# Value products of two quads in one run, with single-quad value loads, in a cross-attention kernel on one core

## The chip, the cores and the metric

The kernel runs on one core of a Trainium2 chip. The core has a matrix engine (TensorE, "PE" in the profile; its weight loads are "PEld"), VectorE (DVE), ScalarE (ACT), GpSimd (POOL), and SyncE (SP), which here only issues transfers (DMAs). The engines run at the same time, each through its own list in order, and wait for one another by semaphores. The metric is the device time of one execution in microseconds (us), lower is better.

## The reference

Layer norm, cross-attention with 32 heads of 32 channels, output projection, residual; all in float32. B = 8 batches, S = 256 query rows, T = 256 context rows, D = 1024. The context serves as keys and as values, and is not projected.

```
x = (hidden - mean) * rsqrt(var + 1e-5) * gamma + beta
Q = split_heads(x @ Wq.T)                    # 8 x 32 x 256 x 32
K = V = split_heads(ctx)
scores = einsum('bhsd,bhtd->bhst', Q, K) * 32 ** -0.5     # masked with -inf
probs = softmax(scores)
attn = einsum('bhst,bhtd->bhsd', probs, V)
out = hidden + attn.reshape(B, S, D) @ Wout.T
```

## The kernel before

The work goes by quads: four heads, that is 128 channels, of one batch. There are 8 quads to a batch and N = 64 in all. The main loop runs over slots n = 0 to 63, and the order in which it issues instructions is the order on each engine; there is no scheduler (`manual_schedule`). What a slot puts on PE, in order:

1. the scores of quad n + 1 (L481, 16 instructions in the profile, into four PSUM banks),
2. steps of the output projection, "place 0" (`project_steps(n, 0)`),
3. the value products of quad n - 2 (L624): for each of four blocks of context rows, four heads and two halves of the rows, a matmul with 64 rows and 32 columns; 64 instructions in the profile, into two PSUM tiles `pv`,
4. steps, "place 1",
5. the query projection for a later quad (L342 in the first two batches; later one of seven block products a slot, L442, 32 instructions in the profile),
6. after the softmax has been issued, steps, "place 2".

The output projection of a batch is done while the next batch is worked on. It is a 2 x 2 block product in seven products (`PRODUCTS`: A11, A12, S2, ...) of four chunks each, 28 steps; a step is one matmul of 128 x 512 (L710), which the profile shows as two. `STEPS` says how many go into places 0, 1 and 2 of the nine slots in which the projection of a batch runs (the ninth is the first of the batch after). In `P1_ASIDE` batches the first product has a PSUM bank of its own. A step needs the attention outputs `at` of its quads, which ACT copies from `pv` (`copy_at`, L637).

In slot n the softmax of quad n + 1 is issued (`softmax_parts`). For each of the four heads DVE adds the mask and takes the minimum (L517), ACT makes the exponentials and their sum (L521), DVE the reciprocals (L528), POOL the scaling (L530), and DVE transposes blocks of 32 into `pT` (L536). ACT copies part of `pT` aside into `pc` (`aside`, L542). At the end stands `tail()`: the last transpose, the last copy aside, and then on SP two moves within `pT` (L602), the loads given as `between`, and two moves from `pc` into `pT` (L606). SP runs these in order: a load in `between` is issued after the moves of L602, which wait for the last copy aside. In the first eight and the last seven quads the tail is put off into the softmax that follows.

`copy_at` stands in the softmax after the first head's exponentials, or after the last head's where `late` is set.

Values are loaded for two quads at a time (`load_v`, 512 KB, two buffers, tile `v`): in an odd slot n for quads n + 1 and n + 2. Keys are loaded for two quads in an even slot (`load_k`, 256 KB). Slots and quads before the change:

```
        if n >= 2:
            values(n - 2)
...
        if n % 2 and n + 1 < N:
            between.append(partial(load_v, n + 1))
        elif n % 2 == 0 and n + 4 < N:
            between.append(partial(load_k, n + 4))
```

`ps_s` (scores) has four PSUM banks, `ps_v` (values) two, the query projection and the output projection one each.

## Time and profile before

| | us |
|---|---|
| median of 3 runs (572.2 to 574.37) | 572.57 |
| the profiled execution | 571.86 |
| its span | 570.1 |
| PE busy | 564.9 (99%) |
| DVE busy | 459.4 (81%) |
| ACT busy | 411.4 (72%) |
| POOL busy | 410.3 (72%) |
| value products, PE (L624, 4096 instructions) | 74.4 |
| scores, PE (L481, 1024 instructions) | 73.6 |

The columns of a timeline line are start, length, engine, line, operation, out<-in with shapes, and how many instructions were merged. Busy time of PE is counted from starts to modelled ends, so neighbouring runs overlap a little; from the start of one run to the start of the next is the cleaner measure of what a run costs. "to landing" of a DMA is from the start of its issue on the queue to the last part's arrival.

### The profile page before, as it was taken

What the parts mean: (1) busy time and instruction counts of PE and PEld (TensorE: products, weight loads), DVE (VectorE), ACT (ScalarE), POOL (GpSimd) and SP (SyncE); (2) the same over time, 40 slices, a digit from 0 to 9 for tenths busy, and PEclk for the clock granted to TensorE, in tenths of its full rate; (3) what the DMA queues carried; (4) which work ended last, traced back from release to release, by engine and by line L of the source; (5) the groups of instructions that cost most, each with busy time, mean ns of one, the idle gap of its engine ahead of it and who ended that gap; (6) DMA issues with size and microseconds to landing.
All of it is one profiled execution on the core that took longest, in us unless ns stands there. A gap on an engine that the chain in (4) does not pass through costs nothing.

```text
span 570.1 us, 19996 instructions
## 1 busy us (share of the span) xinstructions
PE 564.9 (99%) x7162; PEld 392.0 (69%) x7162; DVE 459.4 (81%) x1695; ACT 411.4 (72%) x1425; POOL 410.3 (72%) x677
## 2 busy tenths in 40 slices
PE   8999999999999999999999999999999999999997
PEld 8788885666667777667776777667766767755544
DVE  5897988797878888978898888988888877879823
ACT  4698887776768857787667867778766876769820
POOL 1788898899887896866569566677648657448780
PEclk9999999999999999999999999999999999999999
DMA  8973777756777767877788767886568864536751
GB/s 312 396 216 118 224 203 206 223 159 191 213 237 247 227 188 231 249 207 221 193 241 231 226 175 215 242 271 182 141 176 265 254 196 126 144 111 179 208 159 75
DMA packets 47475, 117.98 MB, mean 207 GB/s; under 512 B 9104, under 2 KB 9872, under 8 KB 47376
## 3 DMA queue, kind: packets, MB, share of 16 engines
q1 hardware_dynamic: 47088, 116.69, 68.5%
q8 instruction: 57, 0.93, 0.7%
q14 instruction: 42, 0.34, 0.2%
q10 hardware_dynamic: 288, 0.01, 0.0%
HBM read 65.28 MB, written 11.53 MB: 135 GB/s over the span
## 4 chain that ended last, share of the span: by engine, by line
PE 85%; POOL 6%; DVE 4%; issue 2%; ACT 1%; DMA 1%; DVEq 0%; POOLq 0%; ACTq 0%
PE po_S L710 19%; PE pq_A L442 16%; PE sc L481 11%; PE pv L624 10%; PE po_A L710 10%; PE pq L342 8%; PE pq_S L442 6%; POOL e L530 4%; PE po_end L777 2%; DVE e L517 2%; DVE pT L536 1%; PE po_last L777 1%; PE busy L120 1%; POOL wo L183 1%; ACT e L521 1%
## 5 line engine op out<-in xcount | busy, mean ns | idle before, releaser
L530 POOL TENSOR_SCALAR e<-e,rden 128x256 f32<-128x256 f32 x512 | 236.5, 481 | 116.7 <-DVE rden L528 114.4
L521 ACT ACTIVATE e<-e,mn 128x256 f32<-128x256 f32 x512 | 253.9, 501 | 50.4 <-DVE mn L517 49.3
L536 DVE STREAM_TRANSPOSE pT<-e 128x512 f32<-128x512 f32 x256 | 180.9, 707 | 46.4 <-POOL e L530 38.6
L517 DVE CUSTOM_DVE_ANT_0 e<-sc,mb 128x256 f32<-128x256 f32 x512 | 185.5, 416 | 29.3 <-PE sc L481 28.8
L542 ACT COPY pc<-pT 128x512 f32<-128x512 f32 x128 | 79.1, 618 | 67.2 <-DVE pT L536 38.9
L521 ACT ACTIVATION_READ_ACCUMULATOR e<-e,mn 128x1 f32 x512 | 97.8, 191 | 0.0
L342 PE MATMUL pq<-xnT,wq 128*128 128x256 f32 (+1 forms) x368 | 84.1, 383 | 0.0
L342 PEld LDWEIGHTS pq<-xnT,wq 128*128 128x128 f32 x368 | 68.7, 190 | 14.3 <-issue 4.3
L481 PEld LDWEIGHTS sc<-k,qa 32*128 32x128 f32 x1024 | 46.1, 184 | 42.0 <-issue 20.5
L710 PE MATMUL po_S<-wo,at 128*128 128x512 f32 x152 | 74.5, 607 | 0.4 <-DVE r L752 0.3
L624 PE MATMUL pv<-pT,v 64*32 64x128 f32 x4096 | 74.4, 274 | 0.0
L481 PE MATMUL sc<-k,qa 32*128 32x256 f32 x1024 | 73.6, 400 | 0.1
L624 PEld LDWEIGHTS pv<-pT,v 64*32 64x32 f32 x4096 | 57.0, 105 | 23.1 <-issue 12.5
L710 PE MATMUL po_A<-wo,at 128*128 128x512 f32 x128 | 59.5, 605 | 0.0
L710 PE MATMUL po_S<-wo,s 128*128 128x512 f32 x104 | 49.9, 605 | 0.0
L517 DVE DVE_READ_ACCUMULATOR2_ANT mn<- 128x1 f32 x512 | 42.7, 83 | 0.0
L528 DVE RECIPROCAL rden<-den 128x2 f32<-128x2 f32 x256 | 37.5, 147 | 5.0 <-ACT e L521 4.1
L442 PEld LDWEIGHTS pq_A<-xnT,wq 128*128 128x128 f32 x320 | 37.3, 192 | 4.8 <-issue 4.1
L710 PEld LDWEIGHTS po_A<-wo,at 128*128 128x128 f32 x128 | 22.9, 189 | 25.4 <-issue 24.5
L710 PEld LDWEIGHTS po_S<-wo,at 128*128 128x128 f32 x152 | 25.6, 190 | 20.8 <-issue 19.3
L442 PE MATMUL pq_A<-xnT,wq 128*128 128x128 f32 x320 | 37.3, 275 | 0.0
L637 ACT COPY at<-pv 128x128 f32<-128x128 f32 x128 | 26.2, 253 | 8.7 <-PE pv L624 8.7
(95 smaller groups left out, 610.7 us busy)
## 6 DMA issues: line engine op xcount, KB each, us to landing
v<-in_kv_dram SPq DMA_DIRECT2D x32, 512.0 KB, 4.2
pT<-pT SPq DMA_DIRECT2D x128, 128.0 KB, 2.5
pT<-pc SPq DMA_DIRECT2D x128, 128.0 KB, 4.1
ring<-kept_T SPq DMA_DIRECT2D x18, 512.0 KB, 5.4
k<-in_kv_dram SPq DMA_DIRECT2D x32, 256.0 KB, 4.2
x<-in_x_dram SPq DMA_DIRECT2D x14, 512.0 KB, 5.9
r<-in_x_dram SPq DMA_DIRECT2D x28, 256.0 KB, 4.5
out_dram<-r SPq DMA_DIRECT2D x28, 256.0 KB, 2.8
```

What stands on the lines that cost most here:

```text
L342: nc.tensor.matmul(pqs[n], wq[:, o, c, :], xnTs[b](c), start=(c == 0), stop=(c == NC - 1),)
L442: nc.tensor.matmul(pqs[b][:, o, :], w[:, c], x_[:, c], start=begins and o + c == 0, stop=c == NK - 1, skip_group_check=True,)
L481: nc.tensor.matmul(scs[n][j][:, s, :], qa[r, n % NQ, ts(s, P)], ks[n - n % 2][r, n % 2, :], start=True, stop=True,)
L517: nc.vector.tensor_tensor_reduce(out=e[:, s, :], in0=pss[j][:, s, :], in1=mbs[n // NQ], scale=1.0, scalar=NO_SCORE, op0=ALU.add, op1=ALU.m ...
L521: nc.scalar.activation(e[:, s, :], e[:, s, :], AF.Exp, bias=mn[:, s : s + 1], scale=-1.0, accum_out=den[:, s : s + 1],)
L528: nc.vector.reciprocal(rden, dens[j])
L530: nc.gpsimd.tensor_scalar(es[j][:, s, :], es[j][:, s, :], rden[:, s : s + 1], 1.0, ALU.mult, ALU.mult,)
L536: nc.vector.transpose(pT[:, :, :, j, :, :].rearrange("p a i s k -> p (a i) s k"), es[j].rearrange("p s (b t) -> p b s t", t=K),)
L542: nc.scalar.copy(pc[:, :, ts(j, 2)], pT[:, 1, :, ts(j, 2)])
L624: nc.tensor.matmul(pvs[n][r][j * HD : (j + 1) * HD], vs[n - n % 2][ts(r, 2 * K), i, ds(n % 2 * P + j * HD, HD)], pT[ts(r, 2 * K), :, i, j, ...
L637: nc.scalar.copy(ats[b, k][:, c, :, ts(r, 2), :], pv.rearrange("p a s k -> p s a k"))
L710: nc.tensor.matmul(po, operand(b, name)[:, c], wo[:, which, c], start=begins and c == 0, stop=c == NK - 1, skip_group_check=not begins,)
```

## The change

`values` takes one quad or two. In the odd slots 11 to 55 it runs quads n - 3 and n - 2 one after the other, into the two PSUM tiles, which hold both quads; the even slots 10 to 54 have no value products. Outside them quads run singly as before. `copy_at` copies two quads with one instruction for each half, and is put after the last head's exponentials wherever a pair is waiting. The values of a quad get a tile of their own (256 KB, two buffers), and `v_loads` says in which slot's `between` each is issued: it follows the slot that frees the buffer (`run_at[quad - 2]`), and is one later where that slot has the quad's own number and is one of the pairs'. For pairs from slot 13 on, the even quad q is so loaded in slot q + 1 and the odd quad q also in slot q + 1, and both are used in the pair's slot: q + 3 for the even, q + 2 for the odd. There are four `pT` buffers instead of three and two `pc` instead of three. The host lays each quad's values out together. `STEPS` has other counts in the same 28.

```diff
-    ptp = ctx.enter_context(tc.tile_pool(name="ptp", bufs=3))
-    asp = ctx.enter_context(tc.tile_pool(name="asp", bufs=3))
+    ptp = ctx.enter_context(tc.tile_pool(name="ptp", bufs=4))
+    asp = ctx.enter_context(tc.tile_pool(name="asp", bufs=2))
...
-        vs[n] = vp.tile([P, NI, 2 * P], F32, tag="v", name=f"v_{n}")
+        vs[n] = vp.tile([P, NI, P], F32, tag="v", name=f"v_{n}")
         nc.sync.dma_start(
-            vs[n], kv[b, g // 2, :, 2 * T :].rearrange("p (i v) -> p i v", i=NI)
+            vs[n],
+            kv[b, g // 2, :, ds(2 * T + n % 2 * NI * P, NI * P)].rearrange("p (i v) -> p i v", i=NI),
         )
...
     load_v(0)
+    load_v(1)
...
-            late = "p1" in hooks
+            late = "p1" in hooks or any(len(quads) > 1 for quads in pvs)
...
-    def values(n):
-        pvs[n] = [
-            ps_v.tile([P, 2, NS, K], F32, tag="pv", name=f"pv_{n}_{r}") for r in range(2)
+    def values(*quads):
+        pair = pvs[quads] = [
+            ps_v.tile([P, len(quads), 2, NS, K], F32, tag="pv", name=f"pv_{quads[0]}_{r}")
+            for r in range(2)
         ]
...
+        for at, n in enumerate(quads):
+            pT, v = pTs.pop(n), vs.pop(n)
+            for i in range(NI):
+                for j in range(NH):
+                    for r in range(2):
+                        nc.tensor.matmul(
+                            pair[r][j * HD : (j + 1) * HD, at],
+                            v[ts(r, 2 * K), i, ts(j, HD)],
+                            pT[ts(r, 2 * K), :, i, j, :, :],
+                            start=(i == 0), stop=(i == NI - 1),
+                        )
...
-    STEPS = ((0, 0, 0), (4, 0, 3), (0, 1, 2), (0, 2, 2), (0, 2, 1), (0, 1, 2), (0, 0, 3), (0, 1, 2),
-             (0, 2, 0))
+    STEPS = ((0, 0, 0), (4, 0, 2), (0, 2, 2), (0, 2, 1), (0, 3, 1), (0, 2, 0), (0, 1, 3), (0, 1, 1),
+             (0, 3, 0))
...
-            return STEPS[:1] + ((0, 6, 0), (0, 2, 0), (0, 4, 1), (0, 3, 1)) + STEPS[5:]
-        return STEPS[:1] + ((0, 7, 0),) + STEPS[2:] if b in P1_ASIDE else STEPS
+            return STEPS[:1] + ((0, 6, 0), (0, 2, 1), (0, 3, 1)) + STEPS[4:]
+        return STEPS[:1] + ((0, 6, 0),) + STEPS[2:] if b in P1_ASIDE else STEPS
...
+    PAIRS = range(NQ + 3, N - NQ, 2)
+    runs = {n: (n - 3, n - 2) for n in PAIRS}
+    for n in range(2, N):
+        if not PAIRS[0] - 1 <= n <= PAIRS[-1]:
+            runs[n] = (n - 2,)
+    run_at = {quad: n for n, quads in runs.items() for quad in quads}
+    v_loads = {}
+    for quad in range(2, N):
+        n = max(quad, run_at[quad - 2])
+        n += n == quad and n in PAIRS[:-1]
+        v_loads.setdefault(n, []).append(quad)
...
-        if n % 2 and n + 1 < N:
-            between.append(partial(load_v, n + 1))
-        elif n % 2 == 0 and n + 4 < N:
+        between += [partial(load_v, m) for m in v_loads.get(n, ())]
+        if n % 2 == 0 and n + 4 < N:
             between.append(partial(load_k, n + 4))
...
-        if n >= 2:
-            values(n - 2)
+        if n in runs:
+            values(*runs[n])
```

More of the change, by code (lines that the diff above doesn't have):

```diff
@@ L614, in softmax_parts, with copy_at @@
         yield
-    def values(n):
-        pvs[n] = [
-            ps_v.tile([P, 2, NS, K], F32, tag="pv", name=f"pv_{n}_{r}") for r in range(2)
-        ]
-        pT = pTs.pop(n)
-        for i in range(NI):
-            for j in range(NH):
-                for r in range(2):
-                    nc.tensor.matmul(
-                        pvs[n][r][j * HD : (j + 1) * HD],
-                        vs[n - n % 2][ts(r, 2 * K), i, ds(n % 2 * P + j * HD, HD)],
-                        pT[ts(r, 2 * K), :, i, j, :, :],
-                        start=(i == 0), stop=(i == NI - 1),
-                    )
-    def copy_at(n):
-        b, c = divmod(n, NQ)
+    def values(*quads):
+        pair = pvs[quads] = [
+            ps_v.tile([P, len(quads), 2, NS, K], F32, tag="pv", name=f"pv_{quads[0]}_{r}")
+            for r in range(2)
+        ]
+        for at, n in enumerate(quads):
[9 more added lines that the diff above has]
+                        )
+    def copy_at(quads):
+        b, c = divmod(quads[0], NQ)
         k, c = divmod(c, NK)
@@ L635, in copy_at @@
             ats[b, k] = atp.tile([P, NK, NS, NA, K], F32, tag="at", name=f"at_{b}_{k}")
-        for r, pv in enumerate(pvs.pop(n)):
+        for r, pv in enumerate(pvs.pop(quads)):
             nc.scalar.copy(
-                ats[b, k][:, c, :, ts(r, 2), :], pv.rearrange("p a s k -> p s a k")
+                ats[b, k][:, ds(c, len(quads)), :, ts(r, 2), :],
+                pv.rearrange("p c a s k -> p c s a k"),
             )
@@ L980, in xattn_kernel @@
         else:
-            copy_at(n - 2)
+            copy_at((n - 2,))
             for load in between:
@@ L1057, in xattn_kernel @@
     values(N - 2)
-    copy_at(N - 2)
+    copy_at((N - 2,))
     end_sum(slice(2, 3), nc.gpsimd)
@@ L1065, in xattn_kernel @@
     values(N - 1)
-    copy_at(N - 1)
+    copy_at((N - 1,))
     end_sum(slice(3, 4), nc.vector)
@@ L1106 @@
     keys = keys.transpose(0, 1, 3, 2, 4).reshape(B, D // 256, P, 2 * T)
-    values = v.reshape(B, T // 64, 64, D // 256, 256).transpose(0, 3, 2, 1, 4)
+    values = v.reshape(B, T // 64, 64, D // 256, 2, P).transpose(0, 3, 2, 4, 1, 5)
     values = np.tile(values.reshape(B, D // 256, 64, 4 * T), (1, 1, 2, 1))
```

## The prediction

> **What bounds the kernel now.** First the page: busy times, the slices and the chain that ended last. TensorE (PE) is busy 99% of the span in every slice, at full granted clock, and it is 85% of the chain; no other engine is over 81%.

> ```profile
> span 570.1 us, 19996 instructions
> PE 564.9 (99%) x7162; PEld 392.0 (69%) x7162; DVE 459.4 (81%) x1695; ACT 411.4 (72%) x1425; POOL 410.3 (72%) x677
> PE   8999999999999999999999999999999999999997
> PE 85%; POOL 6%; DVE 4%; issue 2%; ACT 1%; DMA 1%; DVEq 0%; POOLq 0%; ACTq 0%
> ```

> Next the waits of PE alone: they are 2.0 us in all. So the time is the length of PE's own list, and every wait that is put into it is added whole.

> ```profile
> PE busy L120 <- POOL ring masks.py:199: 1.3, 1, 1.3
> PE po_end L777 <- ACT at L637: 0.4, 1, 0.4
> PE po_S L710 <- DVE r L752: 0.3, 1, 0.3
> ```

> Third the timeline of two slots, 28 (even) and 29 (odd), all engines (start, length, what). Slot 28 issues the scores of quad 29 at 254.09. Their softmax ends with the second copy aside (262.86, to 263.49), after which the DMA queue (SP) sends its first moves of the probabilities at 263.52. That is 9.43 us after the scores, and by then PE has begun slot 29 (262.60) and is about to start its value products (263.67). The load that stands between the two pairs of moves, here keys, goes out at 264.71.

> ```profile
> 254.09 1.15 PE L481 MATMUL sc<-k,qa 32*128 32x256 f32 x16
> 255.17 1.16 PE L624 MATMUL pv<-pT,v 64*32 64x128 f32 x64
> 256.25 1.98 PE L710 MATMUL po_S<-wo,at 128*128 128x512 f32 x4
> 258.07 3.73 PE L442 MATMUL pq_A<-xnT,ring 128*128 128x128 f32 x32
> 261.64 1.02 PE L710 MATMUL po_S<-wo,at 128*128 128x512 f32 x2
> 262.60 1.15 PE L481 MATMUL sc<-k,qa 32*128 32x256 f32 x16
> 262.86 0.63 ACT L542 COPY pc<-pT 128x512 f32<-128x512 f32 x1
> 263.52 1.15 SPq L602 DMA_DIRECT2D pT<-pT  x2
> 263.67 1.16 PE L624 MATMUL pv<-pT,v 64*32 64x128 f32 x64
> 264.71 0.58 SPq L136 DMA_DIRECT2D k<-in_kv_dram  x1
> ```

> Last the tile of the keys, whose loads have the size (256 KB) that a value load will have. The line is from the start of the issue to the landing, over 32 loads; 9.1 is the first microseconds of the program, the later ones are 2.8 to 6.2.

> ```profile
> DMA to landing us min/median/max: 2.8/4.2/9.1
> ```

> **The change, part by part.** The sum is made against the profiled execution: span 570.1, its own time 571.86; the median shown, 572.57, is 0.7 higher.

> *Two quads in one run.* From start to next start a scores run costs 1.08 (254.09 to 255.17) and a values run 1.085. The records inside a values run show eight rounds of eight matmuls, 0.109 apart, so 0.873 is work and 0.21 is entering and leaving it. In 23 odd slots (11 to 55) the second quad follows in the same shape: 23 x 0.21 = 4.9 us less. Bounds: nothing, if a run of 128 is limited by issue (late rounds already show single matmuls 0.017 apart, 0.133 for eight), and 4.9. I take 4.9, because the round starts stay 0.109 apart to the end of the run.

> *Steps dealt anew.* One step is two matmuls in the profile, 0.855 us (14 of them take 6.21). Each batch keeps its 28, so nothing is gained or lost; they only level the slots. With 1.08 for scores, 3.57 for a query product and 0.2 for changing shapes, an even slot becomes 1.08 + 4 x 0.855 + 3.57 + 0.2 = 8.27 (7.41 in the first slot of a batch, which has 3), an odd one 8.4 to 9.4. The A12 steps in the third slot now need attention copies that ACT makes after the last exponential: done some 7 us after the odd slot's scores, needed after 8.4 + 1.08. Cover 2.4 us, cost nothing.

> *Copies.* 128 copies of 128 columns (253 ns) become 36 of those and 46 of 256 (nearest row 463 ns, an activation): ACT is 72% busy and nobody waits for it here, so nothing. *Four probability buffers, two copies aside*: with two, the buffer is rewritten about 12 us after its transfers were issued, and those land in 4.1. Nothing.

> *Values by single quads.* This is the part that costs. The even quad of a pair is loaded in the odd slot two before its use. The odd quad q is loaded in slot q + 1, between the moves of the softmax of quad q + 2, and used in slot q + 2. So values of quad 27 are to be loaded where the timeline has keys, at 264.7, by a queue that must first send the moves of quad 29, and are wanted in slot 29, whose run begins at 263.67. The order of SP's queue in the changed program says the same: the load stands directly behind those two moves. Counted from the scores of the even slot:
> - moves sent after 9.74, 9.30, 9.43, 9.34 us in the first, third, fifth and seventh slot of a batch (slots 32, 34, 28, and the end of the copy aside in slot 30),
> - 1.2 for the two issues (263.52 to 264.71), 4.2 to land, 0.1 to restart PE: 5.5;
> - wanted after the even slot, the scores and the first quad of the odd one: 8.27 + 1.08 + 0.87 = 10.22 (first slot 9.36).

> The second quad therefore waits 5.88, 4.58, 4.71 and 4.62 us: 19.8 per batch. Pair 11 has its load a slot earlier; the pairs in 13 to 55 wait, two in the first batch and four in each of five: 9.3 + 99.0 = 108 us. It doesn't shrink from pair to pair, for the next scores stand behind the waiting run on PE and the next load hangs on those scores. Also behind it are the odd slot's steps and product; ACT's two copies of the pair stand ahead of its copies aside, so the odd slot's moves come some 5 us later too, but what they carry is used two slots on. Bounds: a landing of 2.8 gives 22 x 1.4 = 31 less, one of 6.2 gives 44 more; 4.2 is the middle of the same kind of load at the same place in the queue.

> Outside the pairs every single load goes out one slot ahead instead of two. At the end the moves of quad 57 start at 504.57 and the values of quad 56 at 508.97: 504.57 + 1.15 + 4.15 is 0.9 too late. Followed through slots 56 to the end, each wait shifting what comes after, this is about 5 us. At the start (moves at 55.96, wanted at 59.12) it is 2.1 once, about 3 in all, between 1.5 and 5.

> *The clock after a wait.* In the first records of PE 18 matmuls start 0.213 apart and then 0.109: after the idle start it ran at half speed for 3.9 us and lost 18 x 0.104 = 1.9. No row shows PE idle for 4 to 6 us in the middle; waits up to 0.4 left the clock whole. So 0 to 22 x 1.9 = 42 us. The waits lie between the two rows and I take half, 21. [...]

> [...]

> **Sum**: 571.86 - 4.9 + 108 + 5 + 3 + 21 = 704.

> **Rivals.**
> - *On the other side: the values are there in time.* Then only the shape changes count: 571.9 - 4.9 = 567, or 572 if a long run is issue-limited. It decides where moves are sent earlier than 10.22 - 5.4 = 4.8 us after the scores. For it: SP and the DMA queues are not full. Against it: the softmax's last exponential alone ends 6.0 after the scores, in every slot.
> - *No clock loss*: 684. For it: three waits in four are only about 4.6 us, and the first quad's work ends just before each. *Clock lost each time*: 725. For it: the slow start in this trace.
> - *The softmax loop is dragged along*: ACT's copies of the pair wait for the late run and its copy aside and product evacuation come after, at about 13 to 15 us; where this runs into the next even slot's exponentials it delays the moves there too. By the slots' lengths the overlap is 0.2 to 0.4 us in one or two slots of a batch; if it were a whole copy and read (1.3) each time, 22 x 1.3 = 29 more: 733.

> **How the numbers follow.** Late values 0.92: with part of the clock 0.42 (704), without loss 0.25 (684), with all of it 0.17 (725), dragged loop 0.08 (733). In time 0.07 (567 to 572; faster 0.06, within 0.5% 0.01); something that hides nearly all of it 0.01. Low end: 684 with a landing of 2.8 is 653, and 3 less at both ends of the program, 650. High end: 733 with 1.4 us slower landings in each pair, 765. About 0.5% is what a measurement of this kernel can tell from no change.

> **What would show it.** Right: PE's waits list values (L144) or the DMA of v ahead of the value products, 22 times, 4 to 6 us, some 100 us; PE busy near 85%; in the timeline of an odd slot 64 matmuls, a hole, then 64 more, the v load issued about 10.6 us after the even slot's scores. Shape: two quads back to back where nothing waits (slot 11) take 1.96 instead of 2.17. Clock: matmul starts 0.213 apart after the holes, or not. Wrong: runs of 128 without a hole, v landing before 10 us, or a hole whose end is a copy or a probability move instead.

## The result and the profile after

The changed kernel takes 724.09 us (median of 4 runs, 721.64 to 729.01) against 573.17 for the kernel before (4 runs, 572.2 to 574.37): 1.264 times, 95% interval 1.257 to 1.271. The predicted 704 is 20 us short of it; 650 to 765 holds it. The profiled execution has a span of 719.8 us, 149.7 more than before.

Three lines of the page after (span; busy time; busy tenths of PE and of its granted clock in 40 slices), and the shares of the chain that ended last:

```profile
span 719.8 us, 19981 instructions
PE 611.4 (85%) x7162; PEld 420.6 (58%) x7162; DVE 456.7 (63%) x1695; ACT 410.6 (57%) x1379; POOL 410.7 (57%) x677
PE   9998989779976887878978797779777887879988
PEclk9999999989988989999889999889998988999999
PE 65%; DMA 13%; POOL 6%; DVE 5%; issue 4%; ACT 4%; SPq 3%; DVEq 0%; ACTq 0%; POOLq 0%
```

PE has the same 7162 matmuls, yet its busy time grew by 46.5 us and its granted clock is 0.922 in the mean, which was 1.000: the matmuls themselves became longer. The other 103 us of the 149.7 are idle time, and DMA has 13% of the chain, which was 1%. PE's waits say for what (total, times, longest):

```profile
PE pv L628 <- DMA v<-in_kv_dram: 64.7, 17, 5.0
PE pv L628 <- issue: 18.7, 4, 5.8
PE pv L628 <- DMA pT<-pT: 8.9, 2, 5.0
PE pv L628 <- DMA pT<-pc: 4.4, 1, 4.4
PE po_S L715 <- DVE r L757: 3.0, 1, 3.0
```

The first four rows are one thing: all 24 waits stand in front of value products, 17 put down to the values' own load, the rest to whatever event came last by the profile. One odd slot (25) on PE and on SP (start, length, what; idle time ahead in brackets):

```profile
270.61 1.15 PE L483 MATMUL sc<-k,qa 32*128 32x256 f32 x16
271.69 1.16 PE L628 MATMUL pv<-pT,v 64*32 64x128 f32 x64
276.80 2.06 PE L628 MATMUL pv<-pT,v 64*32 64x128 f32 x64 [3.96 <-DMA v<-in_kv_dram]
278.79 5.90 PE L715 MATMUL po_A<-wo,at 128*128 128x512 f32 x12
284.62 1.15 PE L483 MATMUL sc<-k,qa 32*128 32x256 f32 x16
...
272.71 1.15 SPq L604 DMA_DIRECT2D pT<-pT  x2
273.90 0.58 SPq L144 DMA_DIRECT2D v<-in_kv_dram  x1
```

The first quad of the pair runs at 271.69. Only at 272.71 can SP send the moves of the next softmax, at 273.90 the load of the second quad's values, and at 276.80 PE goes on. Then its 64 matmuls take 2.06 us instead of 1.16, and the steps behind them 5.90 instead of 5.42 for the same twelve in e18.

For every run the span can be cut at two places, the start of the scores of quad 13 (slot 12) and of quad 57 (slot 56):

| kernel | time | ratio [95%] | start to 13 | 13 to 57 | 57 to end |
|---|---|---|---|---|---|
| before | 573.17 | 1 | 113.7 | 378.2 | 78.2 |
| after | 724.09 | 1.264 [1.257, 1.271] | 121.9 | 511.1 | 86.8 |
| e1 load in slot q | 596.19 | 1.041 [1.037, 1.044] | 122.9 | 380.4 | 87.8 |
| e2 the late load ahead of the moves | 621.29 | 1.085 [1.083, 1.088] | 120.4 | 411.4 | 87.9 |
| e8 e1, all loads ahead | 590.82 | 1.034 [1.030, 1.038] | 119.6 | 387.3 | 80.5 |
| e7 hole filled | 686.68 | 1.200 [1.195, 1.205] | 122.1 | 476.0 | 88.6 |
| e9 hole half filled | 711.65 | 1.242 [1.238, 1.246] | 123.1 | 501.2 | 88.5 |
| e5 single loads, no pairs | 579.72 | 1.012 [1.011, 1.013] | 120.0 | 377.5 | 80.3 |
| e13 e8, moves of x later | 596.68 | 1.042 [1.039, 1.045] | 114.9 | 398.7 | 80.2 |
| e15 loads on POOL | 581.87 | 1.016 [1.015, 1.018] | 118.0 | 382.6 | 79.3 |
| e16 five slots' loads on POOL | 583.53 | 1.019 [1.016, 1.022] | 118.2 | 385.0 | 79.1 |
| e17 nine slots' loads on POOL | 583.80 | 1.020 [1.015, 1.026] | 115.0 | 391.7 | 79.1 |
| e11 loads on ACT | 580.48 | 1.013 [1.007, 1.019] | 115.7 | 383.2 | 79.1 |
| e18 e11, S2 later everywhere | 571.91 | 0.998 [0.997, 1.000] | 115.3 | 375.5 | 79.1 |

Times are medians; one of e9's four runs (718.93) fell into a slower state of the chip and is left out. The last three columns are of one profiled execution each. Ratios are against runs of the kernel before on the same chip.

### The profile page after: what moved, and what is told of

It reads as the page before. It is cut to its first block, busy times and chain, and to the rows that moved or that the text cites. A ratio compares the mean times of both kernels' runs of the same rounds, so it can differ in the third digit from the quotient of the medians.

```text
span 719.8 us, 19981 instructions
## 1 busy us (share of the span) xinstructions
PE 611.4 (85%) x7162; PEld 420.6 (58%) x7162; DVE 456.7 (63%) x1695; ACT 410.6 (57%) x1379; POOL 410.7 (57%) x677
## 4 chain that ended last, share of the span: by engine, by line
PE 65%; DMA 13%; POOL 6%; DVE 5%; issue 4%; ACT 4%; SPq 3%; DVEq 0%; ACTq 0%; POOLq 0%
PE po_S L715 15%; PE pq_A L444 12%; PE pv L628 8%; PE po_A L715 8%; DMA v<-in_kv_dram 7%; PE pq L344 6%; PE sc L483 6%; PE pq_S L444 5%; POOL e L532 3%; DMA pT<-pT 3%; SPq L604 3%; DVE pT L538 2%; DVE e L519 2%; PE po_end L782 2%; ACT e L523 1%
## 5 line engine op out<-in xcount | busy, mean ns | idle before, releaser
L538 DVE STREAM_TRANSPOSE pT<-e 128x512 f32<-128x512 f32 x256 | 180.8, 707 | 48.1 <-POOL e L532 46.5
L628 PE MATMUL pv<-pT,v 64*32 64x128 f32 x4096 | 92.3, 317 | 100.9 <-DMA v<-in_kv_dram 64.7
L628 PEld LDWEIGHTS pv<-pT,v 64*32 64x32 f32 x4096 | 72.0, 121 | 122.2 <-issue 64.1
L715 PE MATMUL po_S<-wo,at 128*128 128x512 f32 x152 | 82.0, 660 | 0.0
L715 PE MATMUL po_A<-wo,at 128*128 128x512 f32 x128 | 65.5, 656 | 0.0
L641 ACT COPY at<-pv 128x256 f32<-128x256 f32 (+1 forms) x82 | 22.4, 324 | 73.9 <-PE pv L628 73.9
L715 PE MATMUL po_S<-wo,s 128*128 128x512 f32 x104 | 61.4, 720 | 3.0 <-DVE r L757 3.0
L715 PEld LDWEIGHTS po_S<-wo,at 128*128 128x128 f32 x152 | 28.5, 210 | 27.6 <-issue 27.2
L444 PEld LDWEIGHTS pq_A<-xnT,wq 128*128 128x128 f32 x320 | 39.2, 199 | 7.2 <-issue 6.0
L715 PEld LDWEIGHTS po_A<-wo,at 128*128 128x128 f32 x128 | 25.3, 209 | 30.5 <-issue 28.8
```

The source lines that it names most:

```text
L444: nc.tensor.matmul(pqs[b][:, o, :], w[:, c], x_[:, c], start=begins and o + c == 0, stop=c == NK - 1, skip_group_check=True,)
L538: nc.vector.transpose(pT[:, :, :, j, :, :].rearrange("p a i s k -> p (a i) s k"), es[j].rearrange("p s (b t) -> p b s t", t=K),)
L628: nc.tensor.matmul(pair[r][j * HD : (j + 1) * HD, at], v[ts(r, 2 * K), i, ts(j, HD)], pT[ts(r, 2 * K), :, i, j, :, :], start=(i == 0), sto ...
L641: nc.scalar.copy(ats[b, k][:, ds(c, len(quads)), :, ts(r, 2), :], pv.rearrange("p c a s k -> p c s a k"),)
L715: nc.tensor.matmul(po, operand(b, name)[:, c], wo[:, which, c], start=begins and c == 0, stop=c == NK - 1, skip_group_check=not begins,)
```

## The experiments

**e1: is it the slot of the load?** The line that puts the odd quad's load one slot later is dropped; pairs, tiles and steps stay.

```diff
         n = max(quad, run_at[quad - 2])
-        n += n == quad and n in PAIRS[:-1]
         v_loads.setdefault(n, []).append(quad)
```

> The one edit: the odd quad of a pair is loaded one slot earlier, in slot q instead of q + 1, still behind the moves. Theory of the late load: it lands some 15 us after the scores of slot q and is wanted after 18, so the holes inside the 22 runs go, and the slow clock with them: 132.9 us less between the scores of quads 13 and 57, and the pairs' 4.7 us show as a gain. The waits of the singly loaded quads at the start (8.2 us) and the end (8.6) stay in part: about 575 to 583 us, 1 to 2% slower than before. Rival, that the pair's probabilities or its copies are what is late: the holes stay, over 700 us.

596.19 us. Of the 151 us lost, 128 come back with this line. The holes are gone from most of the middle slots, and there one sees what a pair is worth. Odd slot 27 and 29 on PE:

```profile
253.82 2.03 PE L628 MATMUL pv<-pT,v 64*32 64x128 f32 x128
255.79 1.98 PE L715 MATMUL po_S<-wo,s 128*128 128x512 f32 x4
...
270.41 1.15 PE L483 MATMUL sc<-k,qa 32*128 32x256 f32 x16
271.49 0.80 PE L628 MATMUL pv<-pT,v 64*32 64x128 f32 x38
```

The run of 128 costs 255.79 - 253.82 = 1.97. Slots 28 and 29 together take 16.80 instead of 17.02. But the kernel is still 23 us slower than before, and the expectation was missed: 9.2 us are lost at the start, 9.6 at the end (slot 56 alone takes 15.99 instead of 9.37), and the middle, which should have gained 4.9, loses 2.2. In slots 25, 33, 41 and 49 value products still wait (10.4, 10.0, 10.7 and 9.0 us where 8.5 is undisturbed). On SP the loads for slot 25 are sent at 234.05, behind twelve moves of x (L331; the last six are shown) and more, and slot 25 starts at 234.12:

```profile
227.41 3.77 SPq L331 DMA_DIRECT2D xnT<-xe  x6
231.28 0.52 SPq L758 DMA_DIRECT2D out_dram<-r  x1
232.21 1.78 SPq L604 DMA_DIRECT2D pT<-pT  x2
234.05 1.07 SPq L144 DMA_DIRECT2D v<-in_kv_dram  x2
```

These two loads were put into slot 23, which had begun on PE at 218.16. So they go out 15.9 us after the start of their slot; in slot 27, where no moves of x are in the way, it is 11.5.

**e2 and e8: is it the place in SP's list?** In e2 the slot stays as in the change, and the pairs' late load goes ahead of the moves; in e8 e1's slot is taken and all value loads go ahead.

```diff
 e2
+        early = [m for m in v_loads.get(n, ()) if run_at.get(m) == n + 1 and n + 1 in PAIRS]
...
+        ahead = [partial(load_v, m) for m in early] + ahead
 e8
-        n += n == quad and n in PAIRS[:-1]
...
+        ahead = [partial(load_v, m) for m in v_loads.get(n, ())] + ahead
```

> The odd quad's load stays in slot q + 1, but is put on the DMA queue ahead of that slot's moves instead of behind them. Theory of the place in the queue: the load goes out as soon as the previous slot's transfers are issued, some 2 to 5 us after the even slot's scores instead of 10.5, lands by 5 to 9 us, before 10.23 where it is wanted; holes gone but for a few where six moves of x stand ahead; 575 to 590 us. Rival, that one slot is too short for the load wherever it stands: holes of 2 us or more in most pairs, over 640 us.

> The load of the odd quad in slot q, and every value load ahead of the slot's moves, the single ones at the start and the end too. Theory of the late loads: no value product waits, PE is the bound again, and what is left of the change is 23 pairs at 0.21 us: 571.9 - 4.8 = 567 us, faster than before by 0.8% (565 to 569). Rival, that a run of two quads is limited by issue and gains nothing: 572. Rival, that the dealt steps, the later copies or fewer copies aside cost something of their own: 573 to 580, with waits of PE for ACT or DVE.

621.29 and 590.82: both missed, in the same manner. In e2 the pairs that follow the third and fifth slots of a batch have their undisturbed 9.4 and 8.5 us in all but slots 37 and 43 (10.7 and 10.3), so there the moves of the probabilities had been the whole cause. The pairs that follow the seventh slots take 13.1 to 16.4 (but for slot 55, which has 8.6), because the queue is then late with moves of x that belong to slots before. Slot 23 on PE in e2:

```profile
221.43 1.16 PE L628 MATMUL pv<-pT,v 64*32 64x128 f32 x64
227.12 2.06 PE L628 MATMUL pv<-pT,v 64*32 64x128 f32 x64 [4.54 <-DMA v<-in_kv_dram]
```

In e8 the load for slot 25 is out at 231.93 and wanted at 233.8, again behind the moves of x (226.78, 4.15 long); slot 25 takes 12.71 and slot 49 14.43. So the first theory, "the load stands behind two moves", holds only for the place that the prediction looked at. The load is also behind everything else that SP has not yet sent.

**e7 and e9: what does the clock cost?** Between the two quads, nine (e7) or four (e9) matmuls of 128 x 256 keep PE busy while it would wait.

```diff
+            if at and n > 9:
+                for _ in range(9):        # e9: 4
+                    nc.tensor.matmul(
+                        banks[0][:, 256:512], wo[:, B11, 0, :P], wo[:, B11, 0, 0:256],
+                        start=True, stop=True, skip_group_check=True,
+                    )
```

> The changed kernel, with nine matmuls of 256 columns that nobody reads put between the two quads of each run from slot 11 on, about 4.0 us, nearly the length of the hole. They take no part in the result. Theory, that some 40 us of the loss are the clock halved after the hole: the loads land when they did, but PE stays at full clock, about 38 us less than the changed kernel: 683 to 692 us, granted clock 0.98 or more. Rival, that the slow stretch after the hole is PE's restart or late operands and not the clock: no less than 720 us. If the hole were not what sets the pace, the nine would add 4.0 x 23 = 92 us: 815.

> As the kernel with nine unread matmuls, but four of them, 1.9 us, put between the two quads; 2 to 3.5 us of idle time remain. The matmuls take no part in the result. If the clock falls only after an idle stretch of more than about 3.3 us (the shortest hole after which the changed kernel ran slow was 3.4, the longest after which it did not 3.6), nearly all pairs keep it: as with nine, 684 to 692 us, granted clock above 0.98. If any idle stretch of 2 us or more cools the array, it stays near 715 to 724.

e7 takes 686.68. The values come no earlier (the holes of the 22 pairs add up to 103.4 us, after the change to 98.5), so 724.1 - 686.7 = 37 us are what the slow clock cost, or somewhat more. The page of e7 shows the full clock in every slice (0.997 in the mean):

```profile
span 686.7 us, 20773 instructions
PEclk9999999999999999999999999999999999999999
```

e9, 711.65, gives back only 12 and stands beside the second of its two expectations. With e7 as the measure (from the start of the second quad to the next scores 6.53, 7.53, 6.56 and 6.56 us in the pairs that follow the first, third, fifth and seventh slot), the pairs from slot 13 on, without slot 17, which has four steps ahead of its quads, can be sorted by how long PE idled. In e9: up to 2.0 us, none of 4 lost anything; 2.1 to 2.9 us, 6 of 10 did; 3.0 and more, 7 of 7. Whoever lost, lost 1.5 to 2.7 us. After the change 20 of 21 lost, 1.3 to 2.8 each, 39.7 in all. Three pairs of e9 (slots 35, 53 and 27):

```profile
385.23 1.25 PE L637 MATMUL pv<-pT,v 64*32 64x128 f32 x64 [1.53 <-DMA v<-in_kv_dram]
386.41 1.98 PE L724 MATMUL po_S<-wo,s 128*128 128x512 f32 x4
...
592.90 1.96 PE L637 MATMUL pv<-pT,v 64*32 64x128 f32 x64 [2.12 <-DMA v<-in_kv_dram]
594.79 2.75 PE L724 MATMUL po_S<-wo,at 128*128 128x512 f32 x4
...
295.51 1.78 PE L637 MATMUL pv<-pT,v 64*32 64x128 f32 x64 [3.33 <-DMA v<-in_kv_dram]
297.22 3.05 PE L724 MATMUL po_S<-wo,s 128*128 128x512 f32 x4
```

After 1.53 us the run and its steps have their usual 1.2 and 1.98. After 2.12 and 3.33 they have 2.0 and 2.8, or 1.8 and 3.1. The one that lost nothing after the change (slot 27, below) had idled 3.30, so no single length decides:

```profile
298.42 1.23 PE L628 MATMUL pv<-pT,v 64*32 64x128 f32 x64 [3.30 <-DMA v<-in_kv_dram]
299.59 1.98 PE L715 MATMUL po_S<-wo,s 128*128 128x512 f32 x4
```

What does decide can be read from the granted clock. In every trace here it changes only at points that lie whole multiples of 3.41 us apart. Cut into such stretches, e9 around its wait of 2.12 us and the change around its wait of 3.30 us look like this (the stretch and its length; busy time of PE, PEld, DVE, ACT and POOL with instructions; PE's granted clock; DMA's share and GB/s):

```profile
589.54:592.95 3.41, 1.29 (x13) 0.84 (x16) 2.79 (x15) 2.82 (x12) 2.83 (x7) 1.00 0.64 195
592.95:596.36 3.41, 3.41 (x66) 2.29 (x67) 0.67 (x1) 1.17 (x3) 3.29 (x4) 0.50 0.34 85
...
293.44:296.85 3.41, 1.69 (x76) 1.09 (x68) 2.79 (x16) 3.41 (x11) 0.63 (x2) 1.00 0.89 274
296.85:300.26 3.41, 1.84 (x66) 1.40 (x67) 0.11 (x2) 2.40 (x10) 0.55 (x2) 1.00 0.81 257
300.26:303.68 3.42, 3.42 (x25) 2.70 (x24) 1.59 (x5) 0.08 (x1) 1.14 (x3) 1.00 0.04 12
```

The 2.12 us lie inside one stretch and leave PE idle for 62% of it, and the next stretch runs at half clock; the 3.30 us are shared by two stretches, 51% and 46% idle, and the clock stays full. Over all 14 traces, from 12 us on, a stretch at full clock that PE idled for more than 56% was followed by half clock every time (53 times, 22 of them after the change), and one that it idled for less than 52% never was; of four between, two were. So a wait of 1.78 us in e5 (its stretch 52% idle) cost the clock, and one of 2.81 us in e9 (slot 25) did not.

**e5: single loads alone.** The kernel before with each quad's values loaded by themselves in slot q, between the moves, without pairs and with the old steps and buffers.

```diff
...
-        if n % 2 and n + 1 < N:
-            between.append(partial(load_v, n + 1))
-        elif n % 2 == 0 and n + 4 < N:
+        if n >= 2:
+            between.append(partial(load_v, n))
+        if n % 2 == 0 and n + 4 < N:
```

> The kernel before, with only the loads changed: values by single quads, two buffers of 256 KB, quad q loaded in slot q and used in slot q + 2; runs of one quad, old steps, old buffers. Theory: in the middle the load lands 15 us after the scores of quad q + 1 and is wanted after 18, so nothing there; where the softmax's tail is put off or late (quads 3 to 6, 56 to 62) it waits, and where six moves of x fill the DMA queue, as e1 and e2 showed. So 578 to 592 us, waits ahead of value products 8 to 20 us in all, none above 4. Rival, that singles are early enough and all waits of the changed kernel come from the pairs: 572.

579.72. The middle is as before (377.5 against 378.2; 8.51 a slot): two loads in place of one, two slots ahead, cost nothing there, and the waits that the moves of x were expected to make did not come. The loss is at the start, 6.3 (slot 5 takes 11.02 instead of 7.54), and at the end, 2.1. So single loads explain part of the losses at both ends, and nothing in the middle. Of the 8.2 us that the change lost at the start, 4.0 are a step of S2 (below), and of its 8.6 at the end most stand in slot 56, which e5 leaves at 9.37.

**e13, e15, e16, e17: a better place for the loads.** All four load the values of a pair in the odd slot before it, as e8 does, and have S2's first step in slot 10 back where the kernel before has it (see e18). e13 also puts the last six moves of x, and two sums, a slot later. e15 issues all value loads of the loop from POOL's queue behind the copies of the pair; e16 those of slots 23, 31, 39, 47 and 55; e17 those of 25, 33, 41 and 49 too.

```diff
 e13 (on e8)
-                moves=tuple(first - 6 + (i + 2) // 6 for i in range(16)),
+                moves=tuple(first - 6 + (i + 2) // 6 + (i > 9) for i in range(16)),
...
-        for slot, name in ((n + 2, "S1"), (n + 2, "S2"), (n + 1, "S4"), (n - 1, "S3")):
+        for slot, name in ((n + 1, "S1"), (n + 1, "S2"), (n + 1, "S4"), (n - 1, "S3")):
 e15, at the end of copy_at (e16, e17: if n + 2 in ON_POOL)
+        for n in quads:
+            if n + 2 < N:
+                load_v(n + 2, nc.gpsimd)
 all four
-            return STEPS[:1] + ((0, 6, 0), (0, 2, 1), (0, 3, 1)) + STEPS[4:]
+            return STEPS[:1] + ((0, 6, 0), (0, 2, 0), (0, 4, 1)) + STEPS[4:]
```

> e8, with the last six of the 16 moves of x one slot later (behind the value loads of the seventh odd slot on the DMA queue), the first two sums of x one slot later to follow them, and the first batch's S2 step back in its old slot. Theory, that e8's remaining waits are the value loads of one pair in four, stuck behind those moves on SP (issued at 231.9, wanted at 233.8), and the wait of the first S2 step for DVE (3.0 us, and the clock after it): both go, 567 to 571 us. Rival, that the moves only push the next transfers late instead (the tails, and sums of x that POOL waits for): 575 or more, with PE waiting for x parts or scores' banks.

> The changed kernel with its value loads issued by POOL instead of SP, at the place where the copies free the buffers, for quads q + 2, and the first batch's S2 step back in its old slot. Theory of the DMA queue: nothing of SP's order stands ahead of the loads any more; no value product waits for v; what is left is the pairs' 0.22 us each: 566 to 569 us, faster than before by 0.6 to 1%. Rival: issuing 64 loads costs POOL 1 us or more each (410 us busy to 475 or more), the scaling of the exponentials comes later and with it the tails and score banks: 574 or more.

> The schedule of the run in which all value loads go ahead of the moves (590.8 us), with two edits: the loads of five odd slots (23, 31, 39, 47 and 55) are issued by POOL behind the copies of the pair, and the step of S2 in the second slot of the first projection (slot 10) goes back to where the kernel before has it. Theory (what is left of the loss are the loads that stand behind the moves of x on SP, and the dealt step that waits for DVE): slots 25, 33, 41 and 49 fall from 12.7, 9.3, 9.6 and 14.4 to 8.46 each (12.2 us), slot 23 loses 1.3, slot 56 about 1.4, the start about 4.1: span 568 to 570, so 569 to 572 in time, the same as the kernel before or up to 0.5% faster. Rival (POOL's issues delay the scaling and with it DVE, as in the run with all loads on POOL): waits of S2's steps for DVE in slots 26, 34, 42 and 50, 0.4 to 2 us each, and 572 to 576. Rival (another transfer on SP is late once PE is faster): waits for the kept values or for moves of the probabilities appear, 575 or more.

> As the run with five odd slots' loads on POOL (583.5 us), with the loads of slots 25, 33, 41 and 49 on POOL as well. Theory (the ring loads of slots 26, 42 and 50 were late because two more loads of values stood ahead of them on SP): the waits for the kept values go, 5.8, 2.8 and 1.8 us there, with the wait for S2's steps 0.4 to 2 us in some of these slots: 573 to 578. Rival (the ring loads are late whatever the value loads do, as SP is still behind with the moves of x): 580 to 584, the waits for kept values stay.

None reached the forecast; in time each stands in the range of a rival. In e16 and e17 the rival's reason holds too. In e13 what PE waited for most was not parts of x or banks of the scores, as the rival had it, but the kept weights, and in e15 an issue cost POOL 0.58 us (0.78 at most), not the 1 us or more that the rival supposed. In e13 slots 25, 33 and 41 are mended or nearly so (9.40, 8.46, 8.60; slot 49 still takes 11.17), and the next transfer on SP is late:

```profile
PE pq_S L444 <- DMA ring<-kept_T: 9.5, 4, 3.6
```

That is the kept weights, in slots 26, 34, 42 and 50 (15.22, 11.38, 12.91 and 11.21 us, undisturbed 8.28). e16 has the same wait (5.1 us, three times; slot 26 takes 14.07), and so has e17 (6.8, three times), whose theory, that two loads fewer on SP would free it, fell with that. In e15 no value product waits; PE waits for S2's steps (3.0 us, four times) and slot 27 takes 10.26, while POOL's busy time is 443.5 instead of 410 us for 62 loads. In all four the removal of one wait showed the one behind it.

**e11 and e18: loads on ACT, and the dealt steps.** In e11 ACT issues the loads at the same place as POOL in e15. In e18 S2's first steps are, in all later batches too, not the last of the third slot but the middle of the fourth.

```diff
 e11
+                load_v(n + 2, nc.scalar)
 e18 (on e11)
-    STEPS = ((0, 0, 0), (4, 0, 2), (0, 2, 2), (0, 2, 1), (0, 3, 1), ...
+    STEPS = ((0, 0, 0), (4, 0, 2), (0, 2, 0), (0, 4, 1), (0, 3, 1), ...
```

> All value loads of the loop are issued by ACT, directly behind its copies of the value products (where the buffers are known to be free), and the step of S2 in slot 10 goes back to where the kernel before has it; the runs of two quads stay. Theory (the loss comes from where a load stands on SP, and each of SP's own transfers is late when more loads stand among them): with no value load on SP and none on POOL no value product, no kept values and no S2 step wait; the pairs keep 0.14 to 0.22 each (3 to 5 us), slot 56 costs 0.9 more and the start up to 1: 567 to 570. Rival (ACT pays for the issues or is held by them: 62 issues of about 0.5 us on an engine that makes every softmax's exponentials): waits of PE for qa, for pT or for v of 5 us and more, 575 to 590.

> The run with all value loads on ACT (580.5 us), with the two first steps of S2 moved from the last place of the third slot to the middle place of the fourth in every later batch too (they were so moved in the first). Theory (what is left there is the new deal of the steps: S2's first step needs the bank of the products before it, which DVE empties only after POOL has added the kept product): the waits of slots 26, 34, 42 and 50 for DVE go, 1.1, 1.6, 1.4 and 2.6 us against 8.28, and the hole in slot 27 may go too (1.5): 571 to 576, so the same as the kernel before to 0.5% slower, with slot 26 and 27 together 17.7. Rival (the empty bank is late whatever the order, or the shorter even slot runs into the softmax): 577 to 583, the wait moves to the next slot's steps or to the kept values.

e11 takes 580.48, in the range of the rival but not for its reason: PE waits neither for v nor for pT, and 0.3 us for qa. Its profile (slot 34) shows what was left. S2's steps are the first into a bank that DVE must have emptied:

```profile
309.76 3.73 PE L444 MATMUL pq_S<-sx,ring 128*128 128x128 f32 x32
314.83 1.98 PE L718 MATMUL po_S<-wo,s 128*128 128x512 f32 x4 [1.34 <-DVE r L760]
```

Slots 26, 34, 42 and 50 take 9.39, 9.88, 9.68 and 10.85 instead of 8.28, and slot 27 11.20 instead of 9.4 (1.5 of it ahead of a query product, put down to issue). With the steps moved, e18 takes 571.91, ratio 0.9983 [0.9966, 1.0000] in 12 runs against 17 of the kernel before. Its span, busy time and PE's waits:

```profile
span 569.8 us, 20035 instructions
PE 563.5 (99%) x7162; PEld 395.5 (69%) x7162; DVE 455.3 (80%) x1695; ACT 407.6 (72%) x1379; POOL 410.0 (72%) x677
...
PE busy L120 <- POOL ring masks.py:199: 1.4, 1, 1.4
PE pv L628 <- issue: 0.5, 1, 0.5
PE pq L344 <- ACT qa L353: 0.5, 1, 0.5
```

Here the change does what pairs can do: 2.7 us less between quads 13 and 57, and 2.4 us more at the two ends. Its pairs have no hole (128 matmuls in one line):

```profile
242.53 1.15 PE L483 MATMUL sc<-k,qa 32*128 32x256 f32 x16
243.61 2.10 PE L628 MATMUL pv<-pT,v 64*32 64x128 f32 x128
245.64 3.70 PE L718 MATMUL po_S<-wo,s 128*128 128x512 f32 x8
```

## Why the prediction was right, and where it was off

*The holes* (108 us): right in mechanism and place, and near in size partly by luck, since errors of the sum cancelled. Between the first quad's run, taken as 0.873 us of work, and the second lie 98.5 us in the 22 pairs. Against the 108.3 of the sum:

- The landing was shorter: from the send of the load to the second quad lie 2.8 to 5.4 us, 3.8 in the mean, where I took 4.3 (4.2 to land and 0.1 to restart, an estimate; in slots 25 and 27 PE started 0.04 us after the landing). That is 11.7 us less.
- The second quad was wanted 10.23 us after the even slot's scores (predicted 10.22; after first slots 9.37, predicted 9.36; 10.1 in the first batch), except in slot 17, where four steps stand ahead of the pair, which the sum left out: 12.9. That is 3.5 us less.
- The loads were sent later, 5.4 us more in all: 7.8 more after the seventh slots, where SP was late and not the softmax (in slot 22 the last copy aside ended after 9.42 us and the moves were sent after 11.12, with six moves of x and an output ahead of them), and 2.4 less in the rest. The moves were sent after 9.0 to 9.8 us, but in five of the six seventh slots after 10.2 to 11.1 (predicted 9.34).

The row of the values after the change is over all 64 loads, and its median is not that of the late ones:

```profile
DMA to landing us min/median/max: 2.7/3.0/10.1
```

The row of the keys before, 4.2, was nearer to their mean, 3.8.

*The clock* (21): the main error, a term of the right kind and half its size. The step said "I take half" of 42. By e7 the loss is 37 us, by the pairs' sum 39.7, and what is left of the middle's 132.9 after the holes and the shapes (132.9 - 98.5 + 4.7) is 39.1. So the whole 42, in which each of the 22 waits pays the 1.9 of the slow start, was right to within 5 us. e9 shows losses from 2.1 us of idling on, so not only long waits pay: in these traces a little over half of one stretch of 3.41 us was enough. Half was taken because the waits lay between two rows of the trace. In their effect they did not lie in the middle: all but slot 17's were beyond 3 us, and there every pair but one paid, 1.3 to 2.8 us.

*The shape* (4.9): the working held. A run of 128 costs 1.97 (predicted 1.96), and e1 has 0.22 us less for two slots. In e18 the same run costs 2.03 from start to start, and slots 20 and 21 save 0.14. Why it is 1.97 in one schedule and 2.03 in another is open.

*Copies, buffers, two aside* (nothing): e18, which has all three, loses nothing in the middle and shows no wait of PE for them.

*Steps dealt anew* (nothing): wrong. In slot 10, S2's first step now comes before DVE has emptied the bank, which made PE wait 3.04 us and run at a granted clock of 0.50 behind it:

```profile
102.47 3.62 PE L344 MATMUL pq<-xnT,wq 128*128 128x256 f32 x16
109.12 2.07 PE L715 MATMUL po_S<-wo,s 128*128 128x512 f32 x2 [3.04 <-DVE r L757]
111.12 1.82 PE L483 MATMUL sc<-k,qa 32*128 32x256 f32 x16
```

The prediction named a cover for the A12 steps (the copies of ACT) and forgot the bank that S2 begins. That is 4.0 of the 5.2 us by which the start went beyond the forecast (8.2 for 3; slot 10 took 11.55 instead of 7.53). In the later batches the same defect shows only once the holes are gone, and e11 against e18 prices it: 8.6 us. So the step of the prediction that failed here is its "nothing is gained or lost".

*The end* (5): 8.6. The working began with quad 56 and reckoned 0.9 for its values. But in slot 56, where the pairs end, the values of quad 54 already came 3.88 us late; that slot went from 9.37 to 15.88, of which 0.9 is a step dealt there, and the stretch from the scores of quad 63 lost 2.0.

Together: 570.1 - 4.7 + 98.5 + 39.1 + 8.2 + 8.6 = 719.8, the span; it closes because 39.1 is what was left over, and -4.7 is the shape as predicted. Of the rivals, "clock lost each time" (725) is the one that happened, but that its figure is met to 1 us is luck: the holes were 9.5 us smaller than its sum had them, and the two ends 8.8 larger. "No clock loss" (684) is what e7 built (686.7). Some sums of the prediction are 1 us off (683 for 684, 764 for 765), which changes nothing. The dragged softmax loop did not happen: the last copy aside ended 9.0 to 9.7 us after the even slot's scores in all 22 pairs. "In time" (567 to 572) did not happen. Shifting the loads within SP's list (e1, e2, e8) did not bring it about either, none got below 590; it took another queue and other steps (e18, 571.9).

## What to carry to other kernels

When a kernel's bound is the length of one engine's list, price each moved load by where its queue really stands at that moment, not by its neighbours in the program: read the times at which the queue sends, and how far it is behind. In this kernel a wait of TensorE of 3 us or more cost about 2 us on top through the clock nearly every time (27 of 28 pairs after the change and in e9, 1.3 to 2.8 us each), and a shorter one sometimes (6 of 10 from 2.1 to 2.9 us in e9); look at the granted clock behind it. A gain of 0.2 us in 22 places, 4.7 in all, is smaller than one late pair, which cost some 6 us here.
